# A graph layer on one core: the list of runs is loaded second and counted ahead of the turns of h rows, its set-up is moved, and two of the last stores change their queue

## The chip, the cores and the metric

The kernel runs on one core of a Trainium2 chip. The metric is the time of one execution on the device, in microseconds (us). The core's engines work side by side, each on its own list of instructions in order: TensorE (PE in the profile, its weight loads PEld), VectorE (DVE), ScalarE (ACT), GpSimd (POOL) and SyncE (SP). SyncE only starts transfers; ScalarE and GpSimd can start them too, and GpSimd alone starts the gathers that take their row numbers from a table. Engines wait for one another through semaphores.

## What is computed

One layer of a graph network on 12500 nodes of 256 features with 200000 edges, sorted by their target `dst`. The targets are dense at low numbers (they are the square of a uniform number times 12500).

```python
h = relu(layernorm(x))
q, k, v = (h @ W + b for each of the three)           # 8 heads of 32 features
logits = sum_d(q[dst] * k[src]) / sqrt(32)             # per edge and head
expv   = exp(logits - segment_max(logits, dst)[dst])
attn   = expv / segment_sum(expv, dst)[dst]
agg    = segment_sum(attn * v[src], dst)
y      = h + gelu(agg + h @ Wskip + bskip)
out    = x + layernorm(y) * gamma + beta
```

## The kernel before

It has three stretches.

**The projection** (`project`, L173 to L389) goes over 98 blocks of 128 nodes. For each block ScalarE normalises x into h, PE turns h (L261) and multiplies by the weights of k and v (L349), ScalarE copies the turned rows (L263), DVE adds the bias (L357), and SP stores h and the joined rows of k and v into the tables `h_tab` and `kv_tab` in memory. Beside it runs **the plan** (`make_plan`, L543): a Python generator that emits, turn by turn, the small steps by which the edges are cut into lists. Each `yield` is a turn; `project` takes one turn of the plan per block (L378 to L384). A `yield n` leaves n blocks to the next turn. `spend` (L858) is a turn that also takes one step from the tables that the walk will read. The order on each engine in this stretch is the order in which the lines are emitted.

The first 16 nodes have so many edges that they are handled apart: not edge by edge, but by a table that says how often each node is a source for each of the 16. For this the plan makes **the list of runs** (`listed_runs` in the plan, L705): it works out for each of 76 runs of up to 128 edges where it starts (L707 to L721), fetches the sources of the runs by an indirect transfer (L724), splits them into a low and a high part on DVE (L733, L734), makes floats of them on ScalarE (L738), pushes what is beyond a run's end out of range (L740), turns the result on PE (L745 on), copies it (L749) and stores it in `run_tab` (L750, L752). It too is a generator, `side`: `next(side)` is called eight times, once per turn of the loop L788 to L791, and its rest is used up after the loop of the source lists (L864 to L873) in the loop L874. The loop of the source lists turns the sources of all other edges into the gathers' row numbers `idx`.

**The walk** (`walk_streams`, L1101) handles all other edges as 8 streams of 64 steps. A step takes 3 tiles of 128 edges from each stream (the last step one). For each tile and stream GpSimd gathers 128 rows of `kv_tab` (256 KB): 24 gathers a step, 1520 in all. The first two steps are gathered by L1466 (`gather`), the others by L1478 (`gather_row`), into 6 buffers of 8 gathers; a buffer is free when the values in it have been weighed (L1616). In a step PE turns the h rows of the nodes that the step's edges can point to (`turn_windows`, L1440) and makes queries of them (`queries`, L1458), spreads the queries to the edges (`spread`, L1530) with a one-hot matrix made by `hot_e` (L1504, L1507); DVE multiplies them with the gathered keys (`times`, L1541) and adds up per head (`total`, L1548); logits are turned (`turn`, L1567), their running maxima taken by two scans (`maxima`, L1579, L1580), exponentials turned back (L1589); DVE weighs the values (`weigh`, L1616), PE adds them up per node (`add_up`, L1639) and SP stores the sums. From step 2 to 50 each step also handles one piece of the table of the first 16 nodes, and from step 15 on it finishes two blocks of nodes.

In the walk `keep` ties each instruction to the one emitted before it on the same engine, SP's transfers too; the gathers are not tied, so one that waits for nothing can be put ahead of one that does.

At the walk's start (L1896 to L1946) SP loads the edge lists `et` of step 0 (`prefetch`), its h rows (`windows`, L1431), the same for step 1, two penalties, `et` of step 2, and then the list of runs into the tile `run_t` (L1691). The counting goes in tiles of 4 runs, 19 in all: `count(n)` (L1908) emits, up to tile n, the marks of a tile on DVE (L1701, two instructions: which of 128 low parts and which of 98 high parts each source is) and 4 matmuls on PE (L1719). Marks have six buffers. The counts stand in one bank (`ag_ps` has one buffer) and are made in four rounds; after each, ScalarE copies them (L1723) before PE can start the next. After the last round SP stores them (L1725), and behind that store on SP come the loads for the dense keys (L1730 to L1734), of which PE needs `h0` (L1739) at the start of step 0 of the main loop. `count(4)` stands behind the queries of step 0, `count(8)` behind its first spread, `count(12)` behind the queries of step 1, `count(14)` behind its `hot_e`, and the rest in the loop of the first two tiles.

**The end** (L2177 to L2311) finishes the last nodes: two pieces `early_two`, whose 8 stores go out from GpSimd (L2297), and two pieces `last`, each of 4 stores (L2311). All stores are issued by the helper line L1300. L2652 is the closing line of the program; the profile puts there each engine's closing waits and its closing drain, at which the engines meet.

Of the kernel before, what the change touches and what calls it, by code (L numbers as in the profile page):

```python
# [542 lines left out]
def make_plan(tc, pool, ep, psum, src, dst, N, HOLDS, NST, NT, dram, ident, flag, idx, d0_row,  # L543
# [4 lines left out]
    nc = tc.nc  # L548
# [25 lines left out]
    runs = pool.tile([P, DENSE + 1], F32, name="runs")  # L574
# [46 lines left out]
    def plan():  # L621
# [83 lines left out]
        def listed_runs():  # L705
            inside = pool.tile([P, DENSE + 1], F32, name="inside")
            nc.vector.tensor_scalar(inside, runs, rowed[:, 0:1], None, op0=OP.is_le)  # L707
            nc.vector.tensor_tensor(inside[:, :DENSE], inside[:, :DENSE], inside[:, 1:],
                                    op=OP.subtract)
            ends = pool.tile([P, 2, DENSE], F32, name="run_ends")  # L710
            nc.vector.scalar_tensor_tensor(ends[:, 0], runs[:, :DENSE], -float(P), tot[:, :DENSE],
                                           op0=OP.mult, op1=OP.add)
            nc.vector.tensor_mul(ends[:, 0], ends[:, 0], inside[:, :DENSE])
            nc.vector.tensor_mul(ends[:, 1], tot[:, 1:], inside[:, :DENSE])
            span = pool.tile([P, 2], F32, name="run_span")
            nc.vector.tensor_reduce(span, ends, AX.X, OP.add)
            nc.vector.scalar_tensor_tensor(span[:, 0:1], rowed[:, 0:1], float(P), span[:, 0:1],
                                           op0=OP.mult, op1=OP.add)
            run_at = pool.tile([P, 1], I32, name="run_at")
            nc.vector.tensor_scalar(run_at, span[:, 0:1], 1.0, None, op0=OP.add)  # L720
            nc.vector.tensor_sub(span[:, 1:2], span[:, 1:2], span[:, 0:1])  # L721
            yield
            run_i = pool.tile([P, P], I32, name="run_i")
            nc.gpsimd.indirect_dma_start(  # L724
                out=run_i, out_offset=None, in_=src_p[:, :],
                in_offset=bass.IndirectOffsetOnAxis(ap=run_at, axis=0))
            off = pool.tile([P, P], F32, name="run_off")
            nc.vector.tensor_scalar(off, lane, span[:, 1:2], float(2 * P), op0=OP.is_ge,
                                    op1=OP.mult)
            yield  # L730
            yield
            two_i = pool.tile([P, SIDE, P], I32, name="two_i")
            nc.vector.tensor_scalar(two_i[:, 0], run_i, P - 1, None, op0=OP.bitwise_and)  # L733
            nc.vector.tensor_scalar(two_i[:, 1], run_i, P.bit_length() - 1, None,  # L734
                                    op0=OP.arith_shift_right)
            yield
            two = pool.tile([P, SIDE, P], F32, name="two_f")
            nc.scalar.copy(two, two_i)  # L738
            yield
            nc.vector.tensor_add(two, two, off[:, None, :].to_broadcast([P, SIDE, P]))  # L740
            nc.vector.tensor_scalar(own, own, rowed[:, 1:2], None, op0=OP.is_equal)
            for _ in range(4):
                yield
            ps = psum.tile([P, SIDE, P], F32, name="ps_w")
            for i in range(SIDE):  # L745
                nc.tensor.transpose(ps[:, i, :], two[:, i, :], ident)
            yield
            turned = pool.tile([P, SIDE, P], F32, name="run_t")
            nc.vector.tensor_copy(turned, ps)  # L749
            nc.gpsimd.dma_start(run_tab[:, :SIDE * NR].rearrange("p (i n) -> p i n", i=SIDE),  # L750
                                turned[:, :, :NR])
            nc.gpsimd.dma_start(run_tab[:, SIDE * NR:], lane)  # L752
            yield
# [104 lines left out]
        def spend(n):  # L858
            for _ in range(n):
                next(behind, None)  # L860
                yield 1

        sf = pool.tile([NST, S, CH], F32, name="sf", tag="dch")
        for s in range(S + 4):  # L864
            if s < S:
                nc.scalar.copy(sf[:, s], sch[:, s])
            if s >= 4:
                ps = psum.tile([P, K, NST], F32, name="ps_i")
                for j in range(K):
                    nc.tensor.transpose(ps[:, j, :], sf[:, s - 4, j * P:(j + 1) * P],  # L870
                                        ident[:NST, :NST])
                nc.vector.tensor_copy(idx[:, s - 4], ps)
            yield from spend(1)  # L873
        for _ in side:  # L874
            yield from spend(1)
# [18 lines left out]
        for i, w in enumerate((WNN, WN)):  # L894
# [26 lines left out]
        nc.vector.tensor_scalar(lead, lead, -1.0, float(P - 1), op0=OP.mult, op1=OP.add)  # L921
        yield from spend(1)
        nc.vector.tensor_copy(done[:, :F - S], d0_row[:, S:])
        nc.vector.tensor_tensor(done3[:, :NST - 1], done3[:, :NST - 1],
                                nn[:, None, :S].to_broadcast([1, NST - 1, S]), op=OP.subtract)
        nc.vector.tensor_copy(done3[:, NST - 1], cnt[:, 0])
        yield from spend(1)
        full = pool.tile([1, F], F32, name="full", tag="ge_t")
        nc.vector.tensor_scalar(full, done, float(P), None, op0=OP.is_ge)
        nc.vector.tensor_tensor(done3, done3, lead[:, None, :].to_broadcast([1, NST, S]), op=OP.add)  # L930
        blk = pool.tile([1, F], I32, name="blk", tag="num")
        nc.vector.tensor_copy(blk, done)
# [8 lines left out]
        one = pool.tile([1, F], F32, name="one", tag="ge_t")  # L941
        nc.vector.memset(one, 1.0)
        gvu = ep.tile([1, 3, F], F32, name="gvu", tag="hd")
        nc.vector.tensor_tensor_scan(gvu[:, 0], one, more_b, 0.0, op0=OP.mult, op1=OP.add)
        nc.vector.tensor_sub(done, done, gvu[:, 0])
        nc.vector.tensor_sub(lead, nn[:, :S], lead)
        yield from spend(2)
# [153 lines left out]
def walk_streams(tc, N, HID, NST, KL, many, ident, idx, d0_row, slot_row, near, near_n, e_tab, pen_tab, h_tab,  # L1101
# [7 lines left out]
    nc = tc.nc  # L1109
# [250 lines left out]
    with ExitStack() as es:  # L1360
# [51 lines left out]
        def prefetch(c):  # L1412

            g = step[c]
            g["et"] = early.tile([6 * S, CH], BF16, name="et")
            keep(nc.sync.dma_start(g["et"], e_tab[c]))
# [9 lines left out]
        def windows(c):  # L1426

            hw = step[c]["hw"] = hold.tile([P, 3, HID], F32, name="hw")
            for s, node in enumerate(nodes(c)):
                i, at, w = where(s)  # L1430
                keep(nc.sync.dma_start(hw[at:at + w, i, :], h_tab[ds(node, w), :]))  # L1431
# [67 lines left out]
        def hot_e(c, i):  # L1499

            if i == 0:
                step[c]["to_e"] = hot.tile([P, S // 2, CH], F32, name="to_e")
            ps = hot_ps.tile([P, S * WN], F32, name="ps_hot")
            keep(nc.tensor.matmul(ps[:, :CH], near[:, i * P:(i + 1) * P], step[c]["et"],  # L1504
                                  start=True, stop=True))
            turns(latest[PE])
            keep(nc.scalar.activation(step[c]["to_e"][:, i, :], ps[:, :CH], AF.Relu, scale=-1.0,  # L1507
                                      bias=ones))
# [180 lines left out]
        def listed_runs():  # L1689
            t = fin.tile([P, SIDE * NR + P], F32, name="run_t", tag="hT", bufs=1)  # L1690
            keep(nc.sync.dma_start(t, run_tab))  # L1691
            return t[:, :SIDE * NR].rearrange("p (i n) -> p i n", i=SIDE), t[:, SIDE * NR:]
# [201 lines left out]
            return Dense(c - ONCE[0], c) if ONCE[0] <= c < ONCE[1] else None  # L1894

        prefetch(0)  # L1896
        windows(0)
        prefetch(1)
        windows(1)
        penalties(0)  # L1900
        penalties(1)
        prefetch(2)
        runs = listed_runs()
        gather(0, 0)
        tiles = [None] * -(-NR // FOUR)
        counts = counted(tiles)
# [1 line left out]
        def count(upto):  # L1908
            nonlocal_next = count.next
            while nonlocal_next is not None and nonlocal_next < upto:  # L1910
                tiles[nonlocal_next] = marks(runs, nonlocal_next)
                nonlocal_next = next(counts, None)
            count.next = nonlocal_next

        count.next = next(counts)
        for i in range(S // 2):
            hot_e(0, i)
        for part in range(2):
            turn_windows(0, part)
            queries(0, part)  # L1920
        gather(0, 1, latest[ACT])
        count(4)
        for half in range(2):
            spread(0, 0, half)
        count(8)
        for part in range(2):
            turn_windows(1, part)
            queries(1, part)
        for j in range(2, K):
            gather(0, j, latest[ACT])  # L1930
        windows(2)
        count(12)
        for i in range(S // 2):
            hot_e(1, i)
        gather(1, 0, latest[ACT])
        count(14)
        for j in range(K - 1):
            for half in range(2):
                times(0, j, half)
                spread(0, j + 1, half)  # L1940
            count(len(tiles) if j else 17)
            gather(1, j + 1, latest[PE])
            total(0, j)
            if j == 0:
                nc.vector.memset(step[0]["kv"][0][0:1, :, HID - HEADS:], 0.0)
            turn(0, j)  # L1946
# [360 lines left out]
        for p in last:  # L2307
            p.inverse()
            p.placed()
            for part in range(4):  # L2310
                p.store(part, nc.sync if p is last[0] else (nc.scalar, nc.gpsimd)[part // 2])  # L2311


def walk_partitions(tc, src, dst, N, NP, HID, ident, flag, q_tab, kv_tab, table, dram):
# [341 lines left out]
```

## Time and profile before

| | us |
|---|---|
| median of 3 timed runs | 2213.75 (2204.95 to 2214.24) |
| the profiled execution | 2211.57 |
| its span, first to last instruction | 2210.0 |
| last bias of the projection (DVE, L357) | 206.98 |
| first gather of the walk (L1466) | 213.5 |
| first gather of L1478 | 287.9 |
| last gather | 2146.4 |
| last store issued (L1300) | 2197.8 |

The span counts from the first to the last instruction of the program; the profiled execution's own time is 1.57 us longer. Over the span PE is busy 84%, DVE 86%, ACT 54%, POOL 72%, and the 16 DMA engines move 267 GB/s.

How to read the rows: in a timeline a row has its start, how long the merged instructions took from first start to last end, engine, line, operation, what is written from what, how many were merged, and in brackets the idle time before and what ended it. SPq, ACTq and POOLq are the sequencers that issue transfers. In a table of stages the columns after the stretch are its length, then busy time and number of instructions of PE, PEld, DVE, ACT and POOL, then the granted clock of TensorE (1 is full), the share of the DMA engines, and GB/s. A row of waits has who waited, for what, total us, times, and the longest. A row of a line's own view has the count, the shortest, median and longest duration in ns, and when the first and last began.

### The profile page before, as it was taken

The page shows a single profiled execution, that of the slowest core. Times are in us where ns is not written, and L with a number is a line of the kernel's source. Part 1 is how long each engine was busy: PE and PEld are TensorE (multiplying, and loading weights), DVE is VectorE, ACT ScalarE, POOL GpSimd, SP SyncE. Part 2 cuts the span into 40 slices and gives each one's busy share as a digit, 9 for nine tenths or more (in the row PEclk, how much of TensorE's full clock was granted, in tenths as well). Part 3 has the DMA queues.
Part 4 walks back from the last instruction along what each step waited for, and adds up shares of the span by engine and source line. Part 5 has one row for each costly group of instructions (what it writes and reads, how often), then busy time and mean ns, then how long its engine had stood idle before and what let it go on. Part 6 is the DMA issues. An engine that isn't in the chain of part 4 may idle for free. (4 is left out here: it accounts for less than half of the span.)

```text
span 2210.0 us, 38447 instructions
## 1 busy us (share of the span) xinstructions
PE 1864.9 (84%) x10881; PEld 1137.5 (51%) x10881; DVE 1900.2 (86%) x2367; ACT 1199.8 (54%) x2793; POOL 1590.3 (72%) x1737
## 2 busy tenths in 40 slices
PE   9998588787787888888898888898988888787876
PEld 4443355454444555555555555555555555454543
DVE  7885678888887889999999899999999999888885
ACT  5763234444433556656666566566566665455553
POOL 4635767777777777777777777777777777777774
PEclk9998679989888999999999999999999999889888
DMA  9877768888888888989888898889898888898883
GB/s 341 299 257 260 224 199 251 250 250 254 249 251 252 270 273 285 289 283 286 285 273 287 283 288 284 283 276 286 283 285 285 282 274 277 270 280 269 260 260 86
DMA packets 307750, 589.92 MB, mean 267 GB/s; under 512 B 60643, under 2 KB 198296, under 8 KB 304582
## 3 DMA queue, kind: packets, MB, share of 16 engines
q0 software_dynamic: 125152, 409.50, 59.4%
q1 hardware_dynamic: 181382, 176.94, 24.5%
q8 instruction: 89, 1.46, 0.3%
q14 instruction: 135, 1.11, 0.2%
q10 hardware_dynamic: 992, 0.92, 0.1%
HBM read 505.52 MB, written 81.63 MB: 266 GB/s over the span
## 5 line engine op out<-in xcount | busy, mean ns | idle before, releaser
L1478 POOL DMA_INDIRECT kv<-kv_tab,idx x1472 | 1408.3, 957 | 459.8 <-issue 227.7
L1541 DVE TENSOR_TENSOR kv<-ps_qe,kv 128x1024 f32<-128x1024 f32 x380 | 457.2, 1219 | 146.8 <-DMA kv<-kv_tab,idx 75.4
L1530 PE MATMUL ps_qe<-qw,to_e 64*128 64x256 f32 x3040 | 463.3, 413 | 27.5 <-DVE kv L1541 27.5
L1548 DVE TENSOR_REDUCE L<-kv 128x64 f32<-128x2048 f32 x190 | 433.6, 2282 | 3.3
L1616 DVE TENSOR_TENSOR vw<-ps_x,kv 128x2048 f32<-128x2048 f32 x188 | 426.9, 2271 | 10.0 <-PE ps_x L1567 9.1
L1530 PEld LDWEIGHTS ps_qe<-qw,to_e 64*128 64x128 f32 x3040 | 315.4, 200 | 99.8 <-issue 37.5
L1458 PE MATMUL ps_hot<-w_q,hwT 128*128 128x256 f32 x768 | 278.3, 516 | 1.2 <-ACT hwT L1444 1.1
L1461 ACT COPY qw<-ps_hot 128x256 f32<-128x256 f32 (+1 forms) x128 | 60.9, 476 | 311.5 <-PE ps_hot L1458 308.0
L1458 PEld LDWEIGHTS ps_hot<-w_q,hwT 128*128 128x128 f32 x768 | 182.6, 253 | 61.5 <-issue 20.2
L1639 PE MATMUL ps_a<-vw,to_n 128*32 128x264 f32 (+1 forms) x2232 | 206.9, 397 | 6.4 <-ACT kv L1656 6.4
L1507 ACT ACTIVATE to_e<-ps_hot,ones 128x384 f32<-128x384 f32 x256 | 147.7, 583 | 88.8 <-PE ps_hot L1504 62.3
L1567 PE MATMUL ps_x<-ident,L 128*64 128x128 f32 x189 | 57.8, 306 | 161.8 <-DVE vw L1616 151.5
L349 PE MATMUL ps_kv<-w_kv,hT 128*128 128x512 f32 x392 | 184.7, 594 | 1.0 <-ACT hT L263 0.7
L1400 ACT ACT_TABLE_LOAD x142 | 182.2, 1283 | 2.6
L1444 ACT COPY hwT<-ps_hot 128x256 f32<-128x256 f32 (+1 forms) x128 | 61.4, 479 | 147.8 <-PE ps_hot L1440 146.1
L1656 ACT COPY kv<-ps_a 1x264 f32<-1x264 f32 x372 | 137.3, 369 | 4.0
L1639 PEld LDWEIGHTS ps_a<-vw,to_n 128*32 128x32 f32 (+1 forms) x2232 | 84.3, 118 | 106.1 <-issue 53.7
L1520 ACT ACTIVATE to_n<-ps_hot,ones 128x384 f32<-128x384 f32 x189 | 107.5, 575 | 25.3 <-PE ps_hot L1517 23.7
L1567 PEld LDWEIGHTS ps_x<-ident,L 128*64 128x64 f32 x189 | 21.6, 114 | 188.2 <-DVE vw L1616 165.9
L1504 PE MATMUL ps_hot<-et,near 48*128 48x384 bf16 x256 | 90.9, 356 | 14.2 <-ACT qw L1461 7.2
L1639 PE MATMUL ps_hot<-vw,to_n 128*64 128x264 f32 x768 | 101.2, 399 | 0.0
L1570 ACT COPY ps_x<-M 64x1 f32<-64x1 f32 x62 | 9.7, 156 | 166.1 <-PE ps_x L1567 166.1
(434 smaller groups left out, 2764.4 us busy)
## 6 DMA issues: line engine op xcount, KB each, us to landing
kv<-kv_tab,idx POOLq DMA_INDIRECT x1520
kv_tab<-kvo SPq DMA_DIRECT2D x23, 1024.0 KB
hw<-h_tab SPq DMA_DIRECT2D x256, 64.0 KB
table<-sums_w SPq DMA_DIRECT2D x252, 61.9 KB
kv<-h_tab SPq DMA_DIRECT2D x98, 128.0 KB
sums<-table SPq DMA_DIRECT2D x94, 132.0 KB
h<-h_tab SPq DMA_DIRECT2D x94, 128.0 KB
x_f<-in_x_dram SPq DMA_DIRECT2D x94, 128.0 KB
```

The costliest lines, as they stand in the source:

```text
L349: nc.tensor.matmul(ps_kv, hT[:, c, :], w_kv[:, c, :], start=c == 0, stop=c == KC - 1)
L1400: keep(nc.scalar.activation(dummy[:, 1:2], dummy[:, 0:1], function))
L1458: keep(nc.tensor.matmul(ps[:, b, :], g["hwT"][:, b, k, :], w_q[:, k, :], start=False, stop=k == KC - 1, skip_group_check=True))
L1478: ins = nc.gpsimd.indirect_dma_start(out=t[:, s, :], out_offset=None, in_=kv_tab[:, :], in_offset=bass.IndirectOffsetOnAxis(ap=idx[:, s, j ...
L1507: keep(nc.scalar.activation(step[c]["to_e"][:, i, :], ps[:, :CH], AF.Relu, scale=-1.0, bias=ones))
L1520: keep(nc.scalar.activation(step[c]["to_n"][:, j, :], ps, AF.Relu, scale=-1.0, bias=ones))
L1530: keep(nc.tensor.matmul(ps[:, b, a, :], g["to_e"][r, 2 * half + a, j * P:(j + 1) * P], g["qw"][r, (half + a) * half, :], start=True, stop= ...
L1541: keep(nc.vector.tensor_tensor(k, g["qe", half].rearrange("p b a d -> p a b d"), k, op=OP.mult))
L1548: keep(nc.vector.tensor_reduce(g["L"][:, j, :].rearrange("p (s h) -> p s h", s=S), g["kv"][j][:, :, :HID].rearrange("p s (h d) -> p s h d" ...
L1616: keep(engine.tensor_tensor(t[:, :, HEADS:].rearrange("p s (h d) -> p s h d", h=HEADS), wj[:, :, :, None].to_broadcast([P, t.shape[1], HEA ...
L1639: keep(nc.tensor.matmul(ps[at:at + w, :], g["to_n"][:, j, i * P + at:i * P + at + w], g["vw"][j][:, s, :], start=j == 0, stop=j == tiles_o ...
L1656: keep(copy(step[c + 1]["kv"][0][0:1, s, HID - HEADS:], ps[at:at + 1, :]))
```

## The change

1. In the plan, the turns between the indirect fetch of the list of runs (L724) and its first use on DVE (L733) become six instead of two. `next(side, None)` is called in each turn of the loop of source lists too, so the rest of the list's set-up falls into that loop and nothing of it is left for the loop L874 behind it. Four new turns are put between the long one-row steps on DVE further down.
2. At the walk's start the list of runs is loaded as SP's second transfer, behind `et` of step 0. `count(4)` stands ahead of the turns of step 0's h rows, `count(8)` ahead of its first spread, `count(12)` ahead of the turns of step 1's h rows; `count(14)` goes, and the first turn of the loop below counts to 16 and not to 17.
3. Of the last piece's four stores, part 2 goes out from ScalarE and part 3 from SP, both from GpSimd before.

```diff
@@ -727,8 +727,8 @@
             off = pool.tile([P, P], F32, name="run_off")
             nc.vector.tensor_scalar(off, lane, span[:, 1:2], float(2 * P), op0=OP.is_ge,
                                     op1=OP.mult)
-            yield
-            yield
+            for _ in range(6):
+                yield
             two_i = pool.tile([P, SIDE, P], I32, name="two_i")
@@ -870,6 +870,7 @@
                 nc.vector.tensor_copy(idx[:, s - 4], ps)
+            next(side, None)
             yield from spend(1)
         for _ in side:
             yield from spend(1)
@@ -921,12 +922,14 @@
         nc.vector.tensor_copy(done[:, :F - S], d0_row[:, S:])
+        yield from spend(1)
         nc.vector.tensor_tensor(done3[:, :NST - 1], done3[:, :NST - 1],
...
         nc.vector.tensor_scalar(full, done, float(P), None, op0=OP.is_ge)
+        yield from spend(1)
         nc.vector.tensor_tensor(done3, done3, lead[:, None, :].to_broadcast([1, NST, S]), op=OP.add)
@@ -941,7 +944,9 @@
         gvu = ep.tile([1, 3, F], F32, name="gvu", tag="hd")
+        yield from spend(1)
         nc.vector.tensor_tensor_scan(gvu[:, 0], one, more_b, 0.0, op0=OP.mult, op1=OP.add)
+        yield from spend(1)
         nc.vector.tensor_sub(done, done, gvu[:, 0])
@@ -1894,13 +1899,13 @@
         prefetch(0)
+        runs = listed_runs()
         windows(0)
         prefetch(1)
         windows(1)
         penalties(0)
         penalties(1)
         prefetch(2)
-        runs = listed_runs()
         gather(0, 0)
@@ -1915,30 +1920,29 @@
         for i in range(S // 2):
             hot_e(0, i)
+        count(4)
         for part in range(2):
             turn_windows(0, part)
             queries(0, part)
         gather(0, 1, latest[ACT])
-        count(4)
+        count(8)
         for half in range(2):
             spread(0, 0, half)
-        count(8)
+        count(12)
         for part in range(2):
             turn_windows(1, part)
             queries(1, part)
...
         windows(2)
-        count(12)
         for i in range(S // 2):
             hot_e(1, i)
         gather(1, 0, latest[ACT])
-        count(14)
         for j in range(K - 1):
             for half in range(2):
                 times(0, j, half)
                 spread(0, j + 1, half)
-            count(len(tiles) if j else 17)
+            count(len(tiles) if j else 16)
@@ -2308,7 +2312,7 @@
             for part in range(4):
-                p.store(part, nc.sync if p is last[0] else (nc.scalar, nc.gpsimd)[part // 2])
+                p.store(part, nc.sync if p is last[0] or part == 3 else nc.scalar)
```

## The prediction

> **What bounds the kernel now.** I read the page first, for the group that carries most time outside TensorE.
>
> ```profile
> span 2210.0 us, 38447 instructions
> ...
> L1478 POOL DMA_INDIRECT kv<-kv_tab,idx x1472 | 1408.3, 957 | 459.8 <-issue 227.7
> ```
>
> The profiled execution took 2211.57 us, so 1.57 lies outside its span; the median of the three timed runs, 2213.75, is 2.18 above it. The group is the walk's gathers on GpSimd. Next came this line alone, the table of stages, and two waits: DVE's in the walk, and GpSimd's.
>
> ```profile
> L1478 POOL DMA_INDIRECT kv<-kv_tab,idx x1472: 940/946/1463, 287.9 to 2146.4; - x184
> ```
>
> ```profile
> 213.00:279.00 66.00, 38.15 (x194) 23.86 (x192) 37.12 (x50) 16.83 (x25) 50.03 (x48) 0.64 0.75 224
> 279.00:288.00 9.00, 6.52 (x27) 4.50 (x27) 8.93 (x8) 3.60 (x10) 0.29 (x2) 0.61 0.23 70
> 288.00:330.00 42.00, 35.91 (x184) 22.89 (x186) 33.24 (x25) 12.76 (x34) 29.67 (x32) 0.72 0.73 219
> 330.00:780.00 450.00, 356.50 (x2247) 218.60 (x2245) 371.04 (x300) 193.08 (x499) 340.45 (x360) 0.90 0.83 253
> ...
> 1680.00:2147.00 467.00, 391.93 (x2444) 245.47 (x2442) 413.49 (x441) 267.55 (x604) 355.20 (x368) 0.91 0.88 274
> ```
>
> ```profile
> DVE kv L1541 <- DMA kv<-kv_tab,idx: 75.4, 66, 3.5
> ```
>
> ```profile
> POOL kv L1478 <- PE ps_x L1567: 25.9, 54, 8.7
> ```
>
> From 330 to 780 GpSimd issues 360 gathers in 450 us, one every 1.25; from 1680 to 2147 one every 1.27; over the whole line 1858.5 us for 1471 steps, 1.263. DVE waits 75.4 us for what they bring. So the walk runs at the pace of the gathers' issue, and its length from its first gather (287.9) to its last (2146.4) is about fixed. What can be won is ahead of 287.9, behind 2146.4, and little between: 32 gathers in 288 to 330 are 2 us short of 1.25 each. Ahead of 287.9 GpSimd stands still for 8.7 us: the sum's largest term has to come from there.
>
> **Part 1, the set-up in the loop of source lists.** The gather of the list (L724) is used by DVE two blocks of the projection later (L733); now six.
>
> ```profile
> DVE two_i L733 <- DMA run_i<-src_p,run_at: 5.2, 1, 5.2
> ```
>
> ```profile
> PE ps_t L261 <- ACT hT L263: 2.3, 1, 2.3
> ...
> PE ps_kv L349 <- DVE kvo L357: 0.3, 1, 0.3
> ```
>
> ```profile
> 80.00:90.00 10.00, 8.42 (x26) 3.72 (x24) 4.00 (x14) 3.41 (x9) 9.13 (x16) 1.00 0.69 265
> 90.00:100.00 10.00, 9.32 (x30) 4.59 (x31) 9.85 (x32) 8.31 (x21) 3.97 (x6) 1.00 0.80 307
> ```
>
> ```profile
> 195.11 0.14 DVE L1020 TENSOR_SCALAR flag<-w 1x1 int32<-1x1 f32 x1
> ```
>
> The waits of DVE and of PE in the projection, two stretches of 10 us, and the plan's last row: DVE stands 5.2 us at L733, the projection's adds and with them ScalarE's copies stand behind it, and PE, busy elsewhere, runs dry: 10 - 8.42 plus 10 - 9.32 is 2.26 us, the 2.3 of the second fence. Four more blocks of about 2 us are 8, more than 5.2, so the stall goes; next late is nothing, as the list is not needed until the walk. Gain 2.3, bounds 0 (the list lands later too) and 2.6 (with the 0.3 of DVE's bursts, which the four new turns break up). The moved steps add no instruction; they fall on a loop where PE sets the pace. Three turns go behind that loop and four come, so the plan ends one block (2 us) later. Its last row, the flag at 195.1, is used when the projection has ended at about 208; without those 12 us of cover it would cost 2. I cost it at nothing.
>
> **Part 2, the list as second load, counting ahead of the h rows.**
>
> ```profile
> 208.48 0.70 SPq L1416 DMA_DIRECT2D et<-e_tab  x1
> ...
> 212.48 0.80 PE L1504 MATMUL ps_hot<-et,near 48*128 48x384 bf16 x2 [5.94 <-DMA et<-e_tab]
> 212.49 4.67 SPq L1431 DMA_DIRECT2D hw<-h_tab  x8
> ...
> 216.00 0.66 PE L1440 MATMUL ps_hot<-ident,hw 128*128 128x128 f32 x2 [1.30 <-DMA hw<-h_tab]
> ...
> 220.62 0.66 PE L1440 MATMUL ps_hot<-ident,hw 128*128 128x128 f32 x2 [0.70 <-DMA hw<-h_tab]
> ...
> 222.01 3.78 PE L1458 MATMUL ps_hot<-w_q,hwT 128*128 128x256 f32 x8 [0.19 <-ACT hwT L1444]
> ...
> 225.50 0.37 SPq L1691 DMA_DIRECT2D run_t<-run_tab x1
> ...
> 230.56 8.72 DVE L1701 TENSOR_TENSOR marks<-run_t 128x512 bf16<-128x512 f32 x16 [20.29 <-DMA hw<-h_tab]
> ...
> 235.44 3.79 PE L1530 MATMUL ps_qe<-qw,to_e 64*128 64x256 f32 x16
> ...
> 239.15 1.26 PE L1719 MATMUL ps_a<-marks 128*128 128x98 bf16 x16
> ...
> 243.46 1.99 PE L1458 MATMUL ps_hot<-w_q,hwT 128*128 128x256 f32 x8 [0.34 <-ACT hwT L1444]
> ...
> 246.35 0.94 POOL L1466 DMA_INDIRECT kv<-kv_tab,idx  x1 [1.42 <-ACT qw L1461]
> ...
> 250.28 2.35 DVE L1541 TENSOR_TENSOR kv<-ps_qe,kv 128x1024 f32<-128x1024 f32 x2
> ...
> 265.39 1.85 ACT L1723 CAST cnt<-ps_a 128x392 int16<-128x392 f32 x1 [5.33 <-PE ps_a L1719]
> ...
> 272.88 0.39 PE L1739 MATMUL ps_hot<-ident,h 16*128 16x16 f32 x2 [5.53 <-DMA h<-h_tab]
> ...
> 278.24 0.95 POOL L1466 DMA_INDIRECT kv<-kv_tab,idx  x1 [0.30 <-issue]
> ...
> 287.90 0.95 POOL L1478 DMA_INDIRECT kv<-kv_tab,idx  x1 [8.71 <-PE ps_x L1567]
> ```
>
> The rows are from the timeline of the walk's start; all times here are in the clock of before. The list is issued behind `et` (done 209.2), 0.37 us in a gap of SP's that lasts to 212.49, so the h rows behind it start at most 0.4 later. From issue to use `et` took 4.0 and the list itself 5.1; I take 4, landing at 213.2. Each tile of marks takes DVE 8.72 / 8 = 1.09. Four: 217.6, their matmuls end at about 218.1, and PE turns h rows then and not at 216.0. The rows it waited 0.7 for are there by now, so the first queries end 1.4 later, 227.2 for 225.8. `count(8)` finds its marks made: 1.26, to 228.5. Marks 8 to 11 wait only for the buffer of tile 4, read at about 227.5: 4 x 1.09, to 232. The spread's 3.79 ends at 232.3. So DVE's first products start at 232, 18 earlier than 250.28; their eight gathers (213.53 on, 1.25 each) are in by then.
>
> PE is the slower one from here. `count(12)` holds the end of the first round of four: PE waits for ScalarE's 1.85 us copy out of the one bank, and is through at 235.2. Turn and queries of step 1 took 5.0 (240.41 to 245.45) on a full clock and 9.1 (216.00 to 225.79 less 0.7) on a half one: the same eight matmuls are 1.99 in the one, 3.78 in the other. On the half clock: 244.3; four `hot_e` 2, 246.3; spread 3.8, 250.1; `count(16)` with the copy of round two 3.2, 253.3; spread 3.8, 257.1; the last counts 0.8 and copy 1.85, 259.7, against 267.24: 7.6 earlier. On the full clock, in the queries alone, 11.7 earlier.
>
> That copy matters beyond its size: the store of the counts, and behind it on SP the loads of the dense keys, wait for it, PE waits for one of these (272.88), and behind PE come the maxima, the weights, and the gather that takes the first freed buffer. From the copy's end to this gather are 287.90 - 267.24 = 20.7 us, which nothing changes: 280.4, or 276.3 on the full clock. The other floor is GpSimd's own: its 48th gather starts at 278.24, less the 1.42 it waited for step 1's queries (0 to 1.4), plus 1.25: 278.1. So the first late gather starts between 278.1 and 280.4. I take 279.2, the middle: gain 8.7, bounds 5 (list lands 4 later) and 9.8. What is then late is the issue of the first 48 gathers itself.
>
> The trace grants 0.64 of the clock in 213 to 279. The Trainium skill (TensorE: Matmul & The Clock Gate, Part 1) says the gate opens after some 3.4 us of sustained activity, and that an idle window closes it. By that, with less idling, step 1's queries would run full and the gather start at its floor: 1.1 us less than my sum; the 1.99 beside 3.78 for the same work agrees.
>
> **Part 3, the last stores.**
>
> The timeline of the end, and what stands on the kernel's closing line:
>
> ```profile
> 2186.40 4.87 POOL L1300 DMA_DIRECT2D out_dram<-kv  x8 [0.21 <-issue]
> ...
> 2195.45 2.78 SPq L1300 DMA_DIRECT2D out_dram<-kv  x4
> ...
> 2196.49 1.30 ACTq L1300 DMA_DIRECT2D out_dram<-kv  x2
> 2197.15 1.04 POOL L1300 DMA_DIRECT2D out_dram<-kv  x2 [5.88 <-DVE kv L1272]
> ```
>
> ```profile
> L2652 POOLq DRAIN  x3: 46/109/7725, 2201.4 to 2209.7; - x3
> L2652 SPq DRAIN  x3: 7/7/13, 2202.3 to 2209.4; - x3
> ```
>
> Two stores leave GpSimd: one goes behind two on ScalarE (ends at 2198.5 for 2197.8), one behind four on SP (2198.95 for 2198.23). That alone costs 0.7. But SP is through with all landings at 2202.4, and the kernel then stands until GpSimd's closing drain, 7.7 us from 2201.4, is over at 2209.1; 0.9 follows. GpSimd reaches the drain 3.2 us behind its last store (2198.2). Without those two its last store ends at 2191.3: drain at 2194.5, over at 2202.2 if it is as long. SP's end, 2202.4 + 0.7, then sets the end: 2203.1 + 0.9 = 2204.0 for 2210.0, gain 6.0. The trace does not show why the drain is long; the two others are 46 and 109 ns. Bounds: -0.7, if it waits for something later than GpSimd's own work, and 6.3. I take 6.0, as nothing else is under way after 2202.4.
>
> Sum: 2.3 + 8.7 + 6.0 = 17.0; 2211.57 - 17.0 = 2194.6. I forecast 2195.
>
> **Rivals.** (A) The drain stays where it is, and a store has only changed its queue: 2211.57 - 11.0 + 0.7 = 2201.3. For it: all stores of the tail are small, and no row ties the drain to them; against it: SP's 2202.4. The Trainium skill speaks for it (DMA: Bandwidth & Descriptors, "Issuing engines are not separate DMA queues": all run on the same DMA engines, only issue time is saved). No row here decides. (B) The list lands late behind the projection's last stores and the h rows: at 218, five more on PE's path, so the gather starts at 284 to 285, gain 3 to 4: about 2200. For it: the 5.1 us of the list's load; against it: `et` landed in 4. A and B together: 2206.5. (C) Slower: PE becomes the bound. From 1680 it is busy 391.9 of 467 at clock 0.91, 25.6 us of a step of 24 gathers (30.5); under 0.76 it needs more than the step. 288 to 330 had 0.72. If the shifted walk were granted 0.75, each of 60 steps would take 0.5 longer: +33, so 2228. Against it: 0.90 and 0.91 in the long stages.
>
> **How the numbers follow.** Forecast 0.58, A 0.23, B 0.11, A with B 0.04, C 0.04. The low end is the sum with 9.8, 6.3, the 2 us of 288 to 330 and some scatter between runs (2204.95 is 8.8 below their median): 2187. The high end takes in A against the median (+2.2) and B: 2205. About 0.5%, 11 us, can be told from no change. The forecast lies past it; A (10.3) and B (11.6) at its edge, so a bit under half of each counts as faster: 0.69; slower is C and a little: 0.05; the rest is 0.26.
>
> **What would show it.** L733 without a wait, and PE full from 80 to 100; `marks` at about 211 (shifted by part 1), first products some 20 earlier than 250.3, L1478's first gather at about 277 with little idle ahead of it and its last 11 earlier than 2146.4; GpSimd's drain starting near 2183 in the new clock, and no 7 us behind SP's last drain. I am wrong if the gather's start moves by under 5, if the pace between first and last differs from 1.263 by over 0.003, or if the drain still ends 11 us behind the last store.

## The result, and the profile after

| kernel | median us (runs) | ratio to before, 95% interval |
|---|---|---|
| after, first timing | 2193.59 (6), before 2213.51 (6) | 0.9918 [0.9892, 0.9944] |
| after, in a later job | 2192.83 (4), before 2215.77 (7) | 0.9895 [0.9878, 0.9911] |

The change makes the kernel 18 to 23 us faster: (1 - 0.9918) x 2213.51 = 18.2 and (1 - 0.9895) x 2215.77 = 23.3. In two of the later jobs the kernel before, too, took 2933.77 and 2948.48 us, with TensorE, VectorE and ScalarE standing for stretches to which the trace gives no cause, so of the six runs timed there mainly short stretches between neighbouring rows are read.

The page of the kernel after, then its line of late gathers alone (lines have moved by five: L1478 is L1483):

```profile
span 2194.6 us, 38451 instructions
...
L1483 POOL DMA_INDIRECT kv<-kv_tab,idx x1472 | 1410.1, 958 | 448.5 <-issue 222.7
```

```profile
L1483 POOL DMA_INDIRECT kv<-kv_tab,idx x1472: 942/946/1466, 277.6 to 2135.0; - x184
```

The first late gather starts at 277.6 for 287.9, 10.3 earlier, the last at 2135.0 for 2146.4, 11.4 earlier; between them 1857.4 us for 1858.5. So nearly all was won ahead of the walk's long part and behind it. The stretches that answer to those of before:

```profile
80.00:90.00 10.00, 10.00 (x32) 4.83 (x31) 8.46 (x30) 7.42 (x18) 9.19 (x16) 1.00 0.99 371
90.00:100.00 10.00, 10.00 (x32) 4.80 (x31) 8.32 (x26) 6.42 (x17) 5.74 (x9) 1.00 0.74 285
277.50:317.50 40.00, 34.46 (x181) 21.26 (x179) 27.86 (x20) 13.04 (x34) 30.27 (x32) 0.70 0.80 244
320.00:770.00 450.00, 353.88 (x2226) 216.85 (x2226) 370.17 (x302) 191.83 (x497) 340.47 (x360) 0.90 0.83 253
1670.00:2136.00 466.00, 393.11 (x2439) 246.38 (x2438) 412.55 (x438) 267.07 (x602) 354.46 (x368) 0.90 0.88 274
```

Busy TensorE is the second figure: full in both rows from 80 to 100, where before had 8.42 and 9.32. In the third row the last busy figure is GpSimd's: the first 32 late gathers (x32) take 40.0 us, 1.25 each. In before the same 32, from 287.8 to 330.7, took 42.9. The pace of the long stages is what it was.

The start of the walk in the kernel after (start, length, engine, line, operation; in brackets the idle time ahead and what ended it):

```profile
206.95 0.32 SPq L1421 DMA_DIRECT2D et<-e_tab  x1
...
209.79 0.32 SPq L1696 DMA_DIRECT2D run_t<-run_tab  x1
...
212.28 8.74 DVE L1706 TENSOR_TENSOR marks<-run_t 128x512 bf16<-128x512 f32 x16 [3.84 <-ACT to_e L1512]
...
230.33 2.35 DVE L1546 TENSOR_TENSOR kv<-ps_qe,kv 128x1024 f32<-128x1024 f32 x2
...
247.64 1.81 ACT L1728 CAST cnt<-ps_a 128x392 int16<-128x392 f32 x1 [2.39 <-PE ps_a L1724]
...
277.60 0.95 POOL L1483 DMA_INDIRECT kv<-kv_tab,idx  x1 [0.30 <-DMA kv<-kv_tab,idx]
```

The list is used 2.5 us after its issue, first products come at 230.3 for 250.3, the last copy of counts ends at 249.5 for 267.2. GpSimd no longer waits ahead of the first late gather: 0.30 is its usual distance, where before had 8.71.

The end, in the timeline and on the closing line:

```profile
2177.41 4.86 POOL L1305 DMA_DIRECT2D out_dram<-kv  x8 [0.21 <-issue]
...
2186.49 3.53 SPq L1305 DMA_DIRECT2D out_dram<-kv  x5
2187.53 2.14 ACTq L1305 DMA_DIRECT2D out_dram<-kv  x3
```

```profile
L2656 POOLq DRAIN  x3: 46/109/7562, 2184.7 to 2194.3; - x3
L2656 SPq DRAIN  x3: 7/7/13, 2193.7 to 2194.0; - x3
```

GpSimd's drain starts 2.4 us behind its last store (2177.41 + 4.86) and is over at 2192.3. From the start of SyncE's last group of stores to the end of the span are 8.1 us; before had 14.6 (2195.45 to 2210.0).

The account of the two profiled executions: 10.3 ahead of the first late gather, 2.9 in the 32 behind it, 1.8 lost again in the rest of the walk, 6.4 at the end, and 2.4 lost between the last gather and SyncE's last stores (51.5 for 49.1): 15.4 in all. The two losses look like scatter between executions: from the 33rd late gather to the last are 1815.6 us in before and 1817.4 in the kernel after, 1814.0 to 1817.9 in the six other profiles outside those two jobs; the second stretch took 53.5 in one of these, the run e2_list below, whose code there is that of before, and 50.5 to 52.5 in the five others.

### The profile page after: what moved, and what is told of

It is laid out like the page before. It is cut to its first block, busy times and chain, and to the rows that moved or that the text cites. A ratio compares the mean times of both kernels' runs of the same rounds, so it can differ in the third digit from the quotient of the medians.

```text
span 2194.6 us, 38451 instructions
## 1 busy us (share of the span) xinstructions
PE 1861.9 (85%) x10881; PEld 1137.7 (52%) x10881; DVE 1901.5 (87%) x2367; ACT 1198.8 (55%) x2793; POOL 1594.1 (73%) x1735
## 5 line engine op out<-in xcount | busy, mean ns | idle before, releaser
L1483 POOL DMA_INDIRECT kv<-kv_tab,idx x1472 | 1410.1, 958 | 448.5 <-issue 222.7
```

Of the source, the lines that this page charges most:

```text
L1483: ins = nc.gpsimd.indirect_dma_start(out=t[:, s, :], out_offset=None, in_=kv_tab[:, :], in_offset=bass.IndirectOffsetOnAxis(ap=idx[:, s, j ...
```

## The experiments

**Each part alone.** Three kernels were the kernel before with one part of the change: the stores, the list with its counts, the set-up. Their edits are the diff's own hunks.

e1_stores:

```
-p.store(part, nc.sync if p is last[0] else (nc.scalar, nc.gpsimd)[part // 2])
+p.store(part, nc.sync if p is last[0] or part == 3 else nc.scalar)
```

> The kernel before with the last stores moved and nothing else. My theory: GpSimd's closing drain follows its own last store. That store ends at about 2191, the drain of some 7.6 us is over by 2202, and SyncE's own end sets the time: 6 us less than before (ratio 0.9973), with 8 us from SyncE's last group of stores to the end of the span (14.6 before). Rival A: the drain stays where it was, and the time is the same to 0.7 us more. The first late gather stays at 288 in both.

2210.30 for 2213.88, ratio 0.9982 [0.9971, 0.9992]: 4.0 us, 1.8 to 6.4. The closing line and the last stores of e1_stores:

```profile
L2652 POOLq DRAIN  x3: 46/109/7562, 2195.2 to 2204.8; - x3
```

```profile
2196.91 3.51 SPq L1300 DMA_DIRECT2D out_dram<-kv  x5
```

The drain is as long, but starts 6.2 earlier than the 2201.4 of before, and from SyncE's stores to the end (2205.1) are 8.2 us for 14.6. Rival A is out. The trace is the sharper witness here: outside the two jobs named above this distance was 13.8 to 14.6 in the four profiles without the part, 8.1 to 8.3 in the four with it, 5.9 between the means.

e2_list:

```
         prefetch(0)
+        runs = listed_runs()
...
         prefetch(2)
-        runs = listed_runs()
...
+        count(4)
         for part in range(2):
             turn_windows(0, part)
             queries(0, part)
         gather(0, 1, latest[ACT])
-        count(4)
+        count(8)
```

(and the later counts as in the diff)

> The kernel before with the list as second load and counted ahead, and nothing else. My theory: the first late gather starts at GpSimd's own floor, 278 to 280 instead of 287.9, with under 1 us of idle ahead of it, and the time falls by 8 to 9 us (ratio 0.996). Rival B: the list lands late, the gather starts at 284 or later and the time falls by 3 to 4. A third view: the 10 us by which the gather moved in the kernel after came from the set-up's shift of the start, and this kernel alone gains under 6.

2201.77, ratio 0.9947 [0.9935, 0.9959]: 11.7 us, 9.1 to 14.4, more than expected. Its walk's start:

```profile
231.81 2.35 DVE L1541 TENSOR_TENSOR kv<-ps_qe,kv 128x1024 f32<-128x1024 f32 x2
...
249.29 1.83 ACT L1723 CAST cnt<-ps_a 128x392 int16<-128x392 f32 x1 [2.39 <-PE ps_a L1719]
...
271.68 0.30 PE L1567 MATMUL ps_x<-ident,L 128*64 128x128 f32 x1 [1.11 <-DVE vw L1622]
...
277.84 0.95 POOL L1478 DMA_INDIRECT kv<-kv_tab,idx  x1 [0.30 <-DMA kv<-kv_tab,idx]
```

TensorE's turn, for which the first late gather waited in before, is done at 272.0, nearly 6 us before GpSimd gets to that gather. So GpSimd's own issue of the first 48 is the bound, with room to spare on TensorE. Rival B is out.

e3_setup:

```
-            yield
-            yield
+            for _ in range(6):
+                yield
...
+            next(side, None)
```

(and the four turns of the plan)

> The kernel before with the set-up in the loop of source lists and nothing else. My theory: TensorE is full from 80 to 100 us, the first load behind the projection is issued 1.5 us earlier (the kernel after has 206.95 for 208.48) and the first late gather moves by as much: 1.5 us less in all, too little for the times to tell, so the trace decides. Rival: the idle time only moves to another place of the projection (the kernel after has 1.5 us of it in 20 to 80), and nothing is left: 0.

2209.06, ratio 0.9978 [0.9965, 0.9991]: 4.9 us, 2.0 to 7.7. Its first load behind the projection, and its late gathers:

```profile
203.84 0.33 SPq L1421 DMA_DIRECT2D et<-e_tab  x1
```

```profile
L1483 POOL DMA_INDIRECT kv<-kv_tab,idx x1472: 941/946/1466, 284.2 to 2147.1; - x184
```

One profile scatters here by the loads of the projection's first 80 us (TensorE stands 0 to 1.5 us between 20 and 80), so I take all fourteen, as this load comes ahead of the stretches without a cause: this load was issued at 207.0 to 208.8 in the six kernels without the part (mean 207.85), at 203.8 to 207.0 in the eight with it (205.51). That is 2.3 us, and 2.4 with the two jobs left out (208.14 and 205.75). The rival, nothing left, is out. In this one profile, of the slowest of its nine executions, the lead shrinks on the way: the first gather is 6 us earlier than in before, the first late gather 3.7, the 33rd late gather 1.6; why was not looked into.

The first gather moves by 3.5 (means of the fourteen, 212.6 and 209.1), 1.2 more than the load. So the load is also used sooner: 4.0 us behind its issue in before, 2.9 in the kernel after. The DMA engines suggest why (before, then the kernel after; the last two figures are their busy share and GB/s):

```profile
200.00:212.00 12.00, 6.54 (x17) 2.64 (x15) 3.27 (x10) 0.37 (x1) 0.00 (x0) 0.89 0.89 323
```

```profile
200.00:212.00 12.00, 7.07 (x19) 2.57 (x17) 3.27 (x10) 1.78 (x4) 1.07 (x1) 0.90 0.71 278
```

They are busy 0.89 of these 12 us in before and 0.71 in the kernel after, so what is moved at the projection's end is through 2.2 us sooner, while the load is issued only 1.5 sooner there. That the load waits behind this traffic fits, but is argued: no run tests it.

The three alone give 4.0 + 11.7 + 4.9 = 20.6 us, the whole 18.2 and 23.3: as far as the intervals tell, the parts add up.

**Which half of the list's part.** e5_early_only is the kernel before with `runs = listed_runs()` behind `prefetch(0)` and the counts where they were.

> The kernel before with the list as second load, the counts where they were. My theory: what cost was VectorE's 20 us wait for the list, so the load alone brings most of it: the first tiles of marks by 218, first products at about 230 instead of 250, the first late gather at 278 to 281, 7 to 9 us less. Rival: the place of the counts carries the gain, since the counts still stand behind queries and spread on TensorE; the load alone moves the gather by 3 us or less.

2207.23, ratio 0.9967 [0.9953, 0.9981]: 7.3 us, 4.2 to 10.4. The start of the walk, and the 32 gathers from the first late one (busy is GpSimd's alone):

```profile
254.05 1.85 ACT L1723 CAST cnt<-ps_a 128x392 int16<-128x392 f32 x1 [5.46 <-PE ps_a L1719]
...
262.81 0.39 PE L1739 MATMUL ps_hot<-ident,h 16*128 16x16 f32 x2 [6.82 <-DMA h<-h_tab]
...
277.35 0.30 PE L1567 MATMUL ps_x<-ident,L 128*64 128x128 f32 x1 [0.76 <-DVE vw L1622]
...
277.90 0.94 POOL L1478 DMA_INDIRECT kv<-kv_tab,idx  x1 [1.33 <-PE ps_x L1567]
```

```profile
277.80:322.70 44.90, 30.22 (x32) 0.67 0.74 213
```

The load alone brings the first late gather to the same place, as my theory had it. But the copy of the counts ends 4.8 later than in e2_list (255.9 for 251.1), GpSimd waits 1.33 us for the turn where 0.30 is its usual distance, and the 32 gathers behind take 44.9 us instead of 40.0. So the counts' place is worth 1.0 at most at the first late gather and 4.9 just behind it: what it buys is TensorE's lead.

**The counts ahead, the list late.** e4_late_list has the counts of e2_list and the list where before loads it.

> The kernel before with the counts ahead of the turns of h rows, but the list loaded where it was. My theory: the two halves of the change hang together. The list is issued at 225.5 and used from 230.6; four tiles of marks take VectorE 4.4, TensorE turns h rows only then, and the queries end at about 245 instead of 225.8. The second group of eight gathers waits for these queries, so GpSimd stands still for some 19 us and the first late gather starts at about 298 instead of 287.9: 8 to 13 us slower (ratio 1.005). Rival: the counts' place alone carries a gain, and the time falls by 2 to 5.

> The same kernel as e4_late_list: the counts ahead of the turns of h rows, the list loaded where it was. The first look fell on a chip where the kernel before too took 2934 us and TensorE stood still for long stretches without a cause in the trace, so the stage in question could not be read. On a chip like that of the first runs my theory stands as it was: queries end at about 245 instead of 225.8, the first late gather at about 298 instead of 287.9, 8 to 13 us slower. Rival: the counts' place alone carries a gain of 2 to 5.

Both ran in the two jobs named above: 2932.93, ratio 0.9990 [0.9953, 1.0028], and 2946.38, 0.9989 [0.9959, 1.0019]. The expectations speak of another chip, which the record does not show: it gives the chip's number as 3 both in the job of e1_stores to e5_early_only and in that of e4_late_list. One of TensorE's waits in e4_late_list (total, times, longest), which the profile of before does not have:

```profile
PE ps_hot L1806 <- issue: 155.8, 32, 10.4
```

VectorE's products stand 377.5 us in all there, 146.8 in before. That hides 10 us, and the price stays unmeasured. The mechanism can be read in e4_again, up to its second group of gathers:

```profile
228.24 8.79 DVE L1701 TENSOR_TENSOR marks<-run_t 128x512 bf16<-128x512 f32 x16 [19.53 <-DMA et<-e_tab]
...
229.53 0.48 PE L1719 MATMUL ps_a<-marks 128*128 128x98 bf16 x4 [16.52 <-DVE marks L1701]
...
242.52 1.30 POOL L1466 DMA_INDIRECT kv<-kv_tab,idx  x1 [11.62 <-ACT qw L1461]
```

TensorE stands 16.5 us for marks whose list is not there (VectorE's row names `et`, the load just ahead of the list; in e4_late_list the same wait, 19.77, is put down to the list itself), the queries end at 241.6 instead of 225.8, and GpSimd stands 11.6 us (I had expected 19): the counts may go ahead of the turns only because the list does.

**The drain.** e6_one_store is the kernel after with `part == 3` of the last pair on `nc.gpsimd`; e7_no_pool_stores has all stores of `early_two` on `nc.sync`.

> The kernel after with one of the two last stores back on GpSimd. My theory: the drain of 7.6 us follows GpSimd's last store, whatever their number, so the whole cost returns: the drain starts 2.4 to 3.2 us behind that store and ends behind everything else, 4 to 6 us more than the kernel after (from SyncE's last group of stores to the span's end 13 to 14.6 us, 8.1 in the kernel after). Rival: the cost goes with the number of stores, half of it returns, 3 us. A third view: the end was set by something else, 0.

> The kernel after with the eight stores ahead of these, which GpSimd still issued, on SyncE as well. One look, for the trace alone. My theory: GpSimd's drain starts some 5 us earlier, behind its last load, and the end does not move, as SyncE's own landings set it already: 8 us from SyncE's last group of stores to the span's end. Rival: the drain still sets the end, and that distance shrinks by up to 5. If the drain belongs to stores and not to loads, it is short here.

Both ran in one of those two jobs (e6_one_store 2930.35, 0.9978 [0.9942, 1.0015]; e7_no_pool_stores one run, 2921.61), so only the last rows count. e6_one_store, span 2924.2:

```profile
2911.28 2.81 SPq L1305 DMA_DIRECT2D out_dram<-kv  x4
2912.32 2.02 ACTq L1305 DMA_DIRECT2D out_dram<-kv  x3
2912.97 0.52 POOL L1305 DMA_DIRECT2D out_dram<-kv  x1 [6.92 <-DVE kv L1277]
```

```profile
L2656 POOLq DRAIN  x3: 46/109/7642, 2915.7 to 2923.9; - x3
```

One store is enough: the drain starts 2.2 behind it, takes 7.6, and the distance from SyncE's stores to the end is 12.9 for 8.1. It goes by the place of GpSimd's last DMA, not by the number. e7_no_pool_stores, span 2919.9:

```profile
2901.70 0.52 POOL L1347 DMA_DIRECT2D kv<-in_x_dram  x1 [0.27 <-issue]
...
2903.55 11.53 SPq L1305 DMA_DIRECT2D out_dram<-kv  x13
```

```profile
L2656 POOLq DRAIN  x3: 46/109/6913, 2904.5 to 2919.6; - x3
```

Behind a load the drain is 6.9 long as well, 2.3 behind it; over at 2911.4, it ends nothing. From the end of SyncE's last store to the end of the span are 4.8 us, 4.6 in the kernel after: SyncE sets the end there already. In all these runs GpSimd's last DMA is also the last work that it does, so they do not tell which of the two the drain follows, and why it is long stays open.

**What holds the first 48 gathers.** In e2_list and the kernel after, GpSimd's own issue had become the bound, and some of these gathers take longer than others. e8_lanes changes what the marks are compared with; SBUF and PSUM, of which its expectation speaks, are the core's two on-chip memories, and without the change both operands of that comparison lie in SBUF:

```
         count.next = next(counts)
+        lanes = logits[:, 512 - P:]
+        keep(nc.scalar.copy(lanes, runs[1]))
+        runs = runs[0], lanes
```

> The kernel after with the row of numbers that the marks are compared with copied into PSUM by ScalarE, so that VectorE's comparison reads one operand from SBUF and one from PSUM. My theory: in the kernel after GpSimd's first 48 gathers took 52.1 us of issue where 48 x 0.95 would be 45.6, since each that meets a marks instruction takes 1.25 to 1.38; the products of the logits, which read one operand from PSUM, do not slow a gather (0.95). So the slow gathers go, the first late gather starts 4 to 6 us earlier relative to the first gather (61 to 63 us behind it, 66.7 in the kernel after), and the time falls by 2 to 5. Rival: the gathers are slowed by something else that runs at the same time, their 1.25 to 1.38 stay, and nothing moves.

> The same kernel as e8_lanes: the kernel after, with the row of numbers of the marks in PSUM; again for a chip like that of the first runs. My theory: no gather takes 1.25 to 1.38 beside a marks instruction any more, the 48 first gathers take about 46 us of issue instead of 50.8 to 52.1, and the first late gather starts 61 to 63 us behind the first instead of 65.5 to 66.7. TensorE's chain was 6 to 8 us ahead of the gathers there, so it becomes the bound at once if more is won, and some of the gain is lost again in the 32 gathers behind: 2 to 5 us less than the kernel after (ratio to before 0.990). Rival: the gathers are slowed by something else, their 1.25 to 1.38 stay, and the time is that of the kernel after (0.992).

> The kernel after itself, beside the next one on the same chip. On a chip like that of the first runs my theory gives 18 to 20 us less than before (ratio 0.991 to 0.992), the first late gather at 277.6, 32 gathers behind it at full pace (40.0 us), and 8 us from SyncE's last group of stores to the end of the span. On a chip where TensorE stands still without a cause in the trace, before at 2930 to 2950, the start and the middle drown in that, and only the end's 6 us are sure: ratio 0.996 to 1.0. Rival: the gain does not depend on the chip, ratio 0.992 there too.

> The kernel after with the marks' row of numbers in PSUM. That no gather is slowed beside the marks any more (0.94 to 0.95 for 1.25 to 1.38) the runs on the other chip have shown; open is what it is worth. My theory, on a chip like that of the first runs: 48 gathers take 45.6 us of issue for 50.8 to 52.1, the first late gather comes 61 to 63 us behind the first (65.5 to 66.7), the time is 2 to 5 us under that of the kernel after. Rival: TensorE's chain is then the bound, the 32 gathers behind lose what was won (over 42 us for 40.0), and the time is that of the kernel after. On a chip where TensorE stands still the two kernels are the same within what can be told.

In the two jobs named above 2924.27, ratio 0.9954 [0.9930, 0.9979], and 2948.71, 0.9990 [0.9963, 1.0016]. In a later job, where before took 2215.77, beside the kernel after: after_again 2192.83, e8_third 2191.66, ratio 0.9887 [0.9868, 0.9905], the same within what can be told. The first 48 gathers and the marks, in the groups of the kernel after and of e8_third (busy, mean ns):

```profile
L1471 POOL DMA_INDIRECT kv<-kv_tab,idx x48 | 52.1, 1085 | 34.9 <-PE ps_hot L1509 20.6 <-issue 11.9 <-DMA kv<-kv_tab,idx 1.8
L1706 DVE TENSOR_TENSOR marks<-run_t 128x512 bf16<-128x512 f32 x19 | 12.9, 680 | 8.8 <-PE ps_a L1724 5.0 <-ACT to_e L1512 3.8
```

```profile
L1471 POOL DMA_INDIRECT kv<-kv_tab,idx x48 | 45.5, 949 | 34.3 <-PE ps_hot L1509 20.0 <-issue 13.1 <-DMA kv<-kv_tab,idx 0.9
L1706 DVE TENSOR_TENSOR marks<-ps_x,run_t 128x512 bf16<-128x512 f32 x19 | 13.0, 684 | 7.6 <-ACT ps_x L1922 3.4 <-PE ps_a L1724 3.1 <-ACT ps_x L1575 1.1
```

The marks are as long as before, and behind the first two gathers (1.07 and 0.99 us in both kernels) each of the 48 takes 0.94 or 0.95: 45.5 us of issue for 52.1 (50.8 in after_again). The first late gather comes 60.7 us behind the first, where after_again has 65.4. And yet nothing is left of it, in e8_third:

```profile
255.31 0.39 PE L1744 MATMUL ps_hot<-ident,h 16*128 16x16 f32 x2 [7.31 <-DMA h<-h_tab]
...
270.34 0.94 POOL L1483 DMA_INDIRECT kv<-kv_tab,idx  x1 [0.89 <-PE ps_x L1572]
```

```profile
270.30:315.30 45.00, 30.26 (x32) 0.66 0.74 216
```

The gather waits for TensorE's turn again, and the 32 behind it take 45.0 for 40.0: the picture of e5_early_only. The rival was right, GpSimd's 4.7 us are given back because TensorE's lead is used up. In that lead lie 7.31 us of waiting for the dense rows of h, whose load stands on SyncE behind the store of the counts. To load them ahead of that store was not tried; it is where I would go on.

## Why the prediction came out right, step by step

**The bound** held: pace 1.263 in before, 1857.4 / 1471 = 1.263 in after, and the gain lies outside it.

**Part 1**, 2.3: held, 2.3 by the load's issue, with DVE's wait at L733 gone and TensorE full from 80 to 100. The plan's later end cost nothing. The first gather gained 1.2 more, because the load was also used sooner; no step of mine has that.

**Part 2**, 8.7. The rows up to the first products came as worked out: first products at 232 in the prediction, 231.8 in e2_list. Then one step failed in its size: I put the turn and queries of step 1, and the spread behind them, on the half clock, and so the last copy of the counts at 259.7. It ended at 251.1 in e2_list (whose walk begins 0.8 earlier than that of before), because TensorE was granted the full clock:

```profile
230.00:240.00 10.00, 6.71 (x45) 4.08 (x42) 10.00 (x15) 4.74 (x8) 8.17 (x7) 1.00 0.71 200
```

```profile
236.39 2.00 PE L1458 MATMUL ps_hot<-w_q,hwT 128*128 128x256 f32 x8 [0.33 <-ACT hwT L1444]
...
240.06 2.04 PE L1530 MATMUL ps_qe<-qw,to_e 64*128 64x256 f32 x16
```

Turn and queries (233.17 to 238.39) took 5.2 us where I had 9.1, the spread 2.04 where I had 3.8: 5.7 of the 7.8 us that are left when the 0.8 is taken off. In before the stretch from 230 to 240 has a clock of 0.50, at about the same busy time (6.44), but 212 to 230 ahead of it had 10.44 busy of 18 us in before and 13.82 in e2_list. The Trainium skill (TensorE: Matmul & The Clock Gate, Part 1) has the gate open after some 3.4 us of sustained activity; by that rule the gather would start at its floor, and the trace agrees. The 20.7 us behind the copy were right: 251.1 + 20.7 is 271.8, the turn ended at 272.0. So TensorE came 6 us early and GpSimd's floor set the start, at 277.8 in e2_list where I had 278.1 for the floor and 279.2 for the start. From first to late gather are 74.4 us in before and 65.5 in e2_list: 8.9. That this is so near 8.7 is luck in part. The 8.7 is the middle between 9.8 by GpSimd's floor and 7.5 by TensorE's chain on the half clock. TensorE's chain was through earlier than in both cases that I worked out, and the floor came 0.9 later than the 9.8 had it: GpSimd's issue of the 48 took 50.8 us for the 50.2 of before, and of the wait of 1.42 that I took off, 0.30 is the usual distance and stays.

The 2 us of 288 to 330, which I kept out of the sum and in the low end of the range, were really won, 2.9 of them, and by the counts' place: e5_early_only loses them and 2 more. The times agree with the rows: 8.9 and 2.9 are 11.8, for 11.7 by the times of e2_list; in e5_early_only 9.1 to the late gather less 2.0 behind it are 7.1, for 7.3.

**Part 3**, 6.0: held, 5.9 by the traces, 4.0 (1.8 to 6.4) by the times of e1_stores. That the drain follows GpSimd's last DMA was a guess from one row; e6_one_store and e7_no_pool_stores show it.

**The rivals.** A fell to the moved drain: its premise from the Trainium skill (DMA: Bandwidth & Descriptors, "Issuing engines are not separate DMA queues"), that a change of the issuing engine saves issue time alone, does not cover the drain that GpSimd runs at the end. B fell to a list used 2.5 us after its issue. C found no foothold, the clock of the long stages stayed at 0.90.

So the sum, 2.3 + 8.7 + 6.0 = 17.0, met 18.2 and 23.3. What it lacked by the traces are the 2.9 in the gathers behind the first late one and the 1.2 of the first gather. The time, 2195 for 2193.59, came nearer than the gain did, and that is luck: the two medians are 19.9 apart, 2.9 more than the sum, but the sum starts from the profiled execution, 1.9 under the median of before.

## What to carry to other kernels

When a stage has two chains that end in the same instruction, the gain of speeding up one stops at the other, and the lead that one chain has over the other is worth something only until it is used up: read both before and after each step. Moving a load early and moving its use early are separate steps: the load alone brought 7.3 us of 11.7 here, the use without the load made TensorE, VectorE and GpSimd wait in turn. At the end of a kernel, look at what each engine does on the closing line: what GpSimd does last, even the issue of a single small store, can set the end.

## What the runs showed of the hardware

- GpSimd closes with a drain of 6.9 to 7.6 us that starts 2.2 to 2.4 us behind its last DMA in the kernel after, e6_one_store and e7_no_pool_stores, be that one store, eight stores or a load (in before 7.7 us, 3.2 behind); SyncE's are 7 to 13 ns.
- In the kernel after a gather's issue takes 0.95 us alone and 1.25 to 1.38, once 3.40, beside the marks, VectorE instructions that read two operands from SBUF; with one of the two in PSUM it takes 0.95 (e8_third), and the marks take about as long (684 ns for 680). The Trainium skill (SBUF — State Buffer, "Who interferes with whom") states that a VectorE instruction with two SBUF inputs contends with a GpSimd instruction that reads SBUF; the gathers' issue agrees with that.
